# A decoder layer's routed experts on one core: gate and up computed by features, with copied weights and later sums

## Chip, core, metric

The kernel runs on one core of a Trainium2 chip. The metric is device time in microseconds (us) from start to end of one execution; lower is better. The profile's engines are TensorE (PE, with its weight loads PEld), VectorE (DVE), ScalarE (ACT), GpSimd (POOL) and SyncE (SP), which issues most DMAs here.

## What is computed

One pre-norm decoder layer over 16 sequences of 256 tokens with 256 features, all in fp32: self-attention with 16 heads, an additive cross term, and a mixture of experts. The change touches only the last of the three:

```python
def _moe(x, gate_w, w_gate, w_up, w_down, ws_gate, ws_up, ws_down):
    shared = silu(x @ ws_gate) * (x @ ws_up) @ ws_down
    scores = sigmoid(x @ gate_w.T)                 # 16 experts
    topk_w, topk_idx = top_k(scores, 2)
    topk_w = topk_w / (topk_w.sum(-1, keepdims=True) + 1e-20) * 2.5
    route = zeros((T, 16)).at[arange(T)[:, None], topk_idx].set(topk_w)
    g = einsum('th,ehm->etm', x, w_gate)           # h = 256, m = 128
    u = einsum('th,ehm->etm', x, w_up)
    eo = einsum('etm,emh->eth', silu(g) * u, w_down)
    return einsum('te,eth->th', route, eo) + shared

x = x + attention(layernorm(x))
x = x + cross(layernorm(x), ctx)
x = x + _moe(layernorm(x), ...)
```

The kernel computes only the two chosen experts of each token. It needs 2 x 4,096 expert rows.

## The kernel before

**First stage (up to some 364 us of the profile).** Attention, the cross term, routing and the shared expert of sequences 0 to 11 run as a software pipeline over the sequences, in an order written out by hand. Every normalised token row (256 features and 8 more columns: two weights, a code of the first expert, the row's number; `ROW` = 264) is scattered twice to a DRAM list, `listed`, so that the rows of one expert stand together in blocks of 128. Blocks are padded to full ones: at most `NB` = 79, of which `USUAL` = 74 are always computed, and the other five only if they are needed (`unusual_blocks`, L1018). `owner_row` holds the expert of each block.

**Block stage.** Class `Block` (L268 to L346) does one block:

- its constructor loads 128 rows of `listed` on SP's queue (132 KB);
- `turn` (L280): two TensorE transposes bring the features to the partitions, ScalarE copies them to `rowsT`;
- `pick` (L288): three VectorE instructions on 128x1 elements choose the row's weight and its destination;
- `hidden_product` (L304): gate and up together. The turned rows are the stationary operand, the expert's weights the moving one, 256 columns (gate and up), two steps of contraction. Tokens lie on the partitions of the result `gu`. ScalarE applies Silu to the gate half;
- `weigh` (L316): VectorE multiplies by the row's weight and by up;
- `turn_hidden` (L323): a third transpose, and VectorE's copy `hidT`, bring the 128 hidden features to the partitions;
- `give` (L329): the down product, ScalarE's copy `got` out of PSUM, and an indirect DMA on GpSimd's queue that scatters the 128 result rows to `given`, one row for each token and choice.

The expert's weights are read from `wgu_sb` and `wd_sb` at an address in a register; `expert_of` (L348) loads the expert numbers of four blocks at a time into TensorE's registers.

**The loop (L1180 to L1206).** Its order is kept as written. Step i does `hidden_product` of block i-2, `turn_hidden` of i-3, `give` of i-4, `turn` of i, `weigh` of i-2, `pick` of i, at most one sum, at a due step one `fetch`, and the row load of block i+9 (`AHEAD`). The first six blocks' rows are loaded before the loop (L1008) into space that is free by then.

**Sums.** `fetch(b)` (L1091) loads both choices of sequence b's 256 tokens from `given` (512 KB, SP's queue), after all scatters up to block `lasts[b]` have landed; the last sequence's comes as two DMAs, one for each tile of 128 tokens. `add` (L1116) adds one 128x256 piece into `x_all` on VectorE; there are four for each sequence. `due` gives the step of each fetch: 25, 29, ... 65 for sequences 0 to 10, then 67, 71, 75, 78, 79. Its sums come `FETCHED` = 6 steps later, one per step. When all of a sequence's sums are done, its output DMA goes out (`added`, L1107).

**Shared expert of the last four sequences.** `SharedLate` (L1123): `gate_up` and `down`. The first `gate_up` stands in step 76, between the last `turn_hidden` and the last `give`s; all else stands behind the loop (L1212 to L1221), with the remaining sums.

PSUM in this stage: two buffers each for `tp`, `gu`, `th` and `eo`. In SBUF, among others, 14 `rows` (one block each), 4 `sum`, 6 `got`.

Of the kernel before, what the change touches and what calls it, by code (L numbers as in the profile page):

```python
# [76 lines left out]
def decoder_kernel(  # L77
# [188 lines left out]
    codes = None  # L266

    class Block:  # L268
        def __init__(self, i, home, rows=None, rowsT=None):
            self.i, self.home, self.rowsT = i, home, rowsT  # L270
            self.rows = self.tile("rows", [P, ROW]) if rows is None else rows
            ins = nc.sync.dma_start(out=self.rows, in_=listed[ts(i, P)])
            behind(ins, enlisted)
            enlisted.clear()
# [13 lines left out]
        def pick(self):  # L288

            code, own = self.rows[:, D + 2 : D + 3], codes[:, self.i : self.i + 1]  # L290
            self.weight = self.tile("weight", [P, 1])
            self.dest = self.tile("dest", [P, 1], I32)
            nc.vector.scalar_tensor_tensor(
                self.weight, code, own, self.rows[:, D : D + 1], ALU.is_equal, ALU.mult
            )
            nc.vector.scalar_tensor_tensor(
                self.dest, code, own, self.rows[:, D + 3 : D + 4], ALU.is_equal, ALU.add
            )

            nc.vector.tensor_tensor(  # L300
                self.weight, self.weight, self.rows[:, D + 1 : D + 2], ALU.max
            )

        def hidden_product(self, e):  # L304
            self.e = e
            gu = self.gu = self.tile("gu", [P, 2 * M])
            for k in range(KT):
                nc.tensor.matmul(  # L308
                    gu, lhsT=self.rowsT[:, k],
                    rhs=wgu_sb[:, ds(e, 1), k].rearrange("p a i m -> p (a i m)"),  # L310
                    start=(k == 0), stop=(k == KT - 1),
                )
            self.hid = self.tile("hid", [P, M])
            nc.scalar.activation(self.hid, gu[:, 0:M], AF.Silu)  # L314

        def weigh(self):  # L316

            nc.vector.scalar_tensor_tensor(  # L318
                self.hid, self.hid, self.weight, self.gu[:, M : 2 * M],
                ALU.mult, ALU.mult,  # L320
            )

        def turn_hidden(self):  # L323
            th = self.tile("th", [P, M])
            nc.tensor.transpose(th, self.hid, ident)  # L325
            self.hidT = self.tile("hidT", [M, P])
            nc.vector.tensor_copy(self.hidT, th)  # L327

        def give(self):  # L329
            eo = self.tile("eo", [P, D])  # L330
            nc.tensor.matmul(  # L331
                eo, lhsT=self.hidT,
# [4 lines left out]
            nc.scalar.copy(got, eo)  # L337
# [10 lines left out]
    def expert_of(i, n=1):  # L348

        _, values = nc.values_load_multi_w_load_instructions(  # L350
            owner_row[:, i : i + n], engines=(mybir.EngineType.PE,), min_val=0, max_val=E - 1,
            skip_runtime_bounds_check_because="a block's owner is one of E experts",
        )
        return values
# [5 lines left out]
    with tc.tile_pool(name="work", bufs=2) as work, tc.tile_pool(  # L360
# [644 lines left out]
        def begin_blocks():  # L1005

            nonlocal codes
            for i in range(6):  # L1008
                rows = h3T[:, i % KT, ds(first_free[i // KT] * TB * P, ROW)]
                blocks.append(Block(i, None, rows))  # L1010
# [7 lines left out]
        def unusual_blocks():  # L1018
# [3 lines left out]
                hidT=(work, "m2", 2), got=(work, "qT", 2), weight=(small, "v2", 4),  # L1022
                dest=(small, "dest", 2), tp=(p_sc, "sc", 2), gu=(p_sc, "sc", 2),
                th=(p_sc, "sc", 2), eo=(p_sc, "sc", 2),
# [5 lines left out]
            with tc.If(used > USUAL):  # L1030
                for i in range(USUAL, NB):
# [3 lines left out]
                    block.hidden_product(expert_of(i)[0])  # L1035
                    block.weigh()
                    block.turn_hidden()
# [49 lines left out]
    with tc.tile_pool(name="ew", bufs=3) as ew, tc.tile_pool(  # L1087
# [3 lines left out]
        def fetch(b):  # L1091

            got = ew.tile([P, TT, 2, D], F32, tag="sum", name="sum", bufs=4)
            parts = [(nc.sync, ts(b, TT), got)]
            if b == B - 1:
# [27 lines left out]
        class SharedLate:  # L1123
# [4 lines left out]

            def gate_up(self):

                ps = p_e.tile([P, 2, T], F32, tag="gu", name="late_ps")
                for i in range(2):
                    for k in range(KT):
                        nc.tensor.matmul(
                            ps[:, i], lhsT=wgu_sb[:, E, k, i], rhs=h3T[:, k, ts(self.b, T)],
                            start=(k == 0), stop=(k == KT - 1),
                        )
                self.hid = ew.tile([P, T], F32, tag="late", name="late", bufs=4)
                nc.scalar.activation(self.hid, ps[:, 0], AF.Silu)
                nc.vector.tensor_tensor(self.hid, self.hid, ps[:, 1], ALU.mult)  # L1140

            def down(self):
                for t in range(TT):
                    eo = p_e.tile([P, D], F32, tag="eo", name="late_eo")
# [10 lines left out]
        AHEAD, LANDED, FETCHED = 9, 3, 6  # L1155
# [4 lines left out]
        for b in range(B):  # L1160
# [3 lines left out]
            step = last + 4 + (LANDED if last + 4 < USUAL - AHEAD else 1)  # L1164
# [6 lines left out]
            rows=(ew, "rows", 14), rowsT=(ew, "rowsT", 3), hid=(ew, "hid", 3), hidT=(ew, "hidT", 3),  # L1171
            got=(ew, "got", 6), weight=(ew, "weight", 4), dest=(ew, "dest", 12), tp=(p_e, "tp", 2),
# [7 lines left out]
        for i in range(max(due) + 1):  # L1180
# [6 lines left out]
            if 3 <= i < USUAL + 3:  # L1187
                blocks[i - 3].turn_hidden()
# [66 lines left out]
```

## Time and profile before

| | |
|---|---|
| median of 6 runs | 508.34 us (505.42 to 509.58) |
| the profiled execution | 508.4 us, span of its instructions 506.6 us |
| mean granted TensorE clock in it | 0.990 |
| first stage, to the first matmul of block 0 | 364.4 us |
| blocks 0 to 73, first gate matmul to the last block's | 120.2 us |
| from there to the end | 22.0 us |

Busy time of each engine in the stretches of the block stage (columns: stretch, its length, then busy us and number of instructions of PE, PEld, DVE, ACT, POOL; the granted clock, the share in which the DMA engines were busy, GB/s):

```profile
372.00:392.00 20.00, 20.00 (x113) 16.91 (x112) 10.91 (x64) 11.55 (x38) 11.66 (x12) 1.00 0.54 167
422.00:432.00 10.00, 10.00 (x57) 8.40 (x56) 7.52 (x38) 5.67 (x19) 6.11 (x7) 1.00 0.88 298
442.00:452.00 10.00, 10.00 (x57) 8.46 (x57) 7.52 (x40) 5.78 (x20) 4.99 (x6) 1.00 0.88 295
452.00:462.00 10.00, 9.22 (x49) 7.28 (x48) 6.50 (x33) 4.80 (x17) 5.97 (x6) 1.00 0.78 244
484.56:506.62 22.06, 13.65 (x61) 10.62 (x59) 13.46 (x38) 3.30 (x9) 4.08 (x5) 0.93 0.55 170
```

A matmul in fp32 shows as two instructions, a transpose as one. Matmuls overlap in their ends, so their pace is read from start to start.

### The profile page before, as it was taken

To read this page: it belongs to the slowest core of one execution; us is meant where nothing else is said; L and a number is where in the kernel's file an instruction comes from. 1 tells how busy PE (TensorE), PEld (TensorE's weight loads), DVE (VectorE), ACT (ScalarE), POOL (GpSimd) and SP (SyncE) were. 2 spreads that over 40 slices of the span, in tenths; PEclk is the share of its full clock that TensorE was granted. 3 is DMA by queue.
4 is the path that set the end of the run, shared out by engine and by line. 5 is a ranking of instruction groups with operands and counts; after the bars stand their busy time and mean duration, and the time that the engine had idled before them with its cause. 6 is when DMAs were issued, how large, how long until landed. Compare 5 with 4: busy or idle time off the path is not lost. (4 is left out here: it accounts for less than half of the span.)

```text
span 506.6 us, 12732 instructions
## 1 busy us (share of the span) xinstructions
PE 472.3 (93%) x4078; PEld 315.6 (62%) x4078; DVE 386.4 (76%) x1607; ACT 329.4 (65%) x783; POOL 321.3 (63%) x539
## 2 busy tenths in 40 slices
PE   1899999999999999999999999998799999999993
PEld 0455656656556556556556655455588888887882
DVE  5845557879989989989989877997655567767765
ACT  2378789888787887888888898221255555555530
POOL 5765345687887887887886655676055566555640
PEclk9999999999999999999999999998899999999998
DMA  7796551342423423320200111112465376978755
GB/s 211 242 343 214 170 170 34 103 130 66 127 84 107 127 82 110 127 97 33 76 34 23 56 41 47 53 45 75 130 204 168 104 243 229 291 250 269 262 159 167
DMA packets 61139, 69.68 MB, mean 138 GB/s; under 512 B 7164, under 2 KB 52493, under 8 KB 61072
## 3 DMA queue, kind: packets, MB, share of 16 engines
q1 hardware_dynamic: 53760, 50.88, 33.2%
q0 software_dynamic: 6624, 17.05, 9.1%
q10 hardware_dynamic: 688, 0.92, 0.5%
q8 instruction: 34, 0.56, 0.4%
q14 instruction: 33, 0.27, 0.2%
HBM read 36.89 MB, written 33.24 MB: 138 GB/s over the span
## 5 line engine op out<-in xcount | busy, mean ns | idle before, releaser
L655 ACT ACTIVATE a<-sc 128x1024 f32<-128x1024 f32 x128 | 124.6, 1030 | 25.2 <-PE sc L645 24.4
L338 POOL DMA_INDIRECT given<-block_got,block_dest x74 | 72.7, 982 | 64.2 <-ACT block_rowsT L286 39.9
L901 POOL DMA_INDIRECT listed<-h,slots x64 | 66.8, 1044 | 16.3 <-issue 15.8
L645 PE MATMUL sc<-qT,kT 32*128 32x256 f32 x1024 | 75.7, 401 | 0.9 <-ACT a L655 0.9
L308 PE MATMUL block_gu<-wgu_sb,block_rowsT 128*128 x288 | 74.4, 381 | 0.3 <-ACT block_rowsT L286 0.3
L645 PEld LDWEIGHTS sc<-qT,kT 32*128 32x128 f32 x1024 | 47.4, 184 | 31.2 <-ACT kT L589 9.1
L665 PE MATMUL av<-a,vaug 128*32 128x256 f32 x1024 | 65.8, 381 | 0.1
L549 PE MATMUL pq<-wqkv,hT 128*128 128x512 f32 x128 | 63.2, 619 | 0.7 <-ACT hT L539 0.7
L327 DVE COPY block_hidT<-block_th 128x128 f32<-128x128 f32 x74 | 21.5, 291 | 41.5 <-PE block_th L325 22.0
L571 POOL TENSOR_TENSOR qkr<-rot,m 128x512 f32<-128x512 f32 x32 | 41.0, 1286 | 17.6 <-DVE m L565 9.5
L308 PEld LDWEIGHTS block_gu<-wgu_sb,block_rowsT 128*128 128x128 f32 x288 | 49.2, 190 | 4.7 <-ACT block_rowsT L286 0.5
L381 POOL TENSOR_TENSOR rs<-rs,neg_half 128x2 f32<-128x2 f32 x64 | 48.1, 752 | 5.3
L331 PE MATMUL block_eo<-wd_sb,block_hidT 128*128 x148 | 44.1, 381 | 0.0
L665 PEld LDWEIGHTS av<-a,vaug 128*32 128x32 f32 x1024 | 29.3, 110 | 21.3 <-issue 6.3
L314 ACT ACTIVATE block_hid<-block_gu 128x128 f32<-128x128 f32 x74 | 20.6, 278 | 33.8 <-PE block_gu L308 12.0
L387 POOL TENSOR_SCALAR h<-x_all,neg,rs 128x256 f32<-128x256 f32 x64 | 40.0, 629 | 3.4
L337 ACT COPY block_got<-block_eo 128x256 f32<-128x256 f32 x74 | 27.5, 372 | 21.3 <-issue 14.1
L676 ACT ACTIVATE xs<-av,vsum 128x256 f32<-128x256 f32 x64 | 27.2, 485 | 16.4 <-PE av L665 16.4
L559 DVE TENSOR_TENSOR rot<-pq,cosf 128x512 f32<-128x512 f32 x32 | 21.9, 686 | 17.3 <-PE pq L549 17.2
L549 PEld LDWEIGHTS pq<-wqkv,hT 128*128 128x128 f32 x128 | 22.6, 196 | 19.0 <-issue 16.7
L529 PE MATMUL tp_h<-ident,h 128*128 128x128 f32 x128 | 19.7, 287 | 11.8 <-POOL h L387 11.7
L597 PE MATMUL pv<-wqkv,hT 128*128 128x256 f32 x128 | 30.4, 380 | 0.1
(190 smaller groups left out, 991.9 us busy)
## 6 DMA issues: line engine op xcount, KB each, us to landing
listed<-empty SPq DMA_DIRECT2D x9, 1056.0 KB
block_rows<-listed SPq DMA_DIRECT2D x68, 132.0 KB
sum<-given SPq DMA_DIRECT2D x15, 512.0 KB
x_all<-in_x_dram SPq DMA_DIRECT2D x16, 256.0 KB
c<-in_ctx_dram SPq DMA_DIRECT2D x16, 256.0 KB
out_dram<-x_all SPq DMA_DIRECT2D x15, 256.0 KB
enc_row<-enc_rows SPq DMA_DIRECT2D x16, 128.0 KB
wgu_sb<-in_L_ffn_w_gate_dram SPq DMA_DIRECT2D x16, 128.0 KB
```

Source lines behind the costliest of these rows:

```text
L308: nc.tensor.matmul(gu, lhsT=self.rowsT[:, k], rhs=wgu_sb[:, ds(e, 1), k].rearrange("p a i m -> p (a i m)"), start=(k == 0), stop=(k == KT ...
L331: nc.tensor.matmul(eo, lhsT=self.hidT, rhs=wd_sb[:, ds(self.e, 1)].rearrange("m a d -> m (a d)"), start=True, stop=True,)
L338: ins = nc.gpsimd.indirect_dma_start(out=given, out_offset=bass.IndirectOffsetOnAxis(ap=self.dest, axis=0), in_=got, in_offset=None, bound ...
L381: nc.gpsimd.tensor_tensor(r, r, neg_half, ALU.pow)
L387: nc.gpsimd.tensor_scalar(h[:, t, 0:D], src[:, t], neg[:, t : t + 1], r[:, t : t + 1], ALU.add, ALU.mult)
L549: nc.tensor.matmul(pq.rearrange("p h i two -> p (h i two)"), lhsT=self.hT[:, k, ts(t, P)], rhs=wqkv[:, k, 0 : 2 * D], start=(k == 0), stop ...
L571: nc.gpsimd.tensor_tensor(self.qkr[:, t], self.rot[t].rearrange("p h d -> p (h d)"), self.m2[t].rearrange("p h i two -> p (h i two)"), ALU ...
L597: nc.tensor.matmul(self.pv[:, t], lhsT=self.hT[:, k, ts(t, P)], rhs=wqkv[:, k, 2 * D : 3 * D], start=(k == 0), stop=(k == KT - 1),)
L645: nc.tensor.matmul(scs[j // 2][:, j % 2, kt], lhsT=self.kT[rows, g % 2, g // 2, ts(kt, P)], rhs=self.qT[rows, g // 2], start=True, stop=True,)
L655: nc.scalar.activation(a, self.scs[g][i], AF.Square, bias=1.0, scale=HD**-0.5)
L665: nc.tensor.matmul(self.av[ts(j, 32), g % 2], lhsT=self.va[:, kt, head], rhs=self.a[g, j // 2][:, j % 2, kt], start=(kt == 0), stop=(kt == ...
L901: ins = nc.gpsimd.indirect_dma_start(out=listed, out_offset=bass.IndirectOffsetOnAxis(ap=self.slots[:, i, t : t + 1], axis=0), in_=self.h3 ...
```

## The change

**Gate and up by features.** `hidden_product` swaps its operands: the expert's weights, 128x128 at a time, are stationary, and the turned rows move, 128 columns. Two halves (gate, up) times two steps of contraction make four matmuls, with hidden features on the partitions of the result. `turn_hidden` and `hidT` go, and so does the step between: `give` of block i-3 now stands in step i.

**Copied weights.** A new `weights` copies the expert's gate and up weights (128x512) on VectorE into a tile `w` with a fixed address (four buffers), in step i for block i. `expert_of` loads the numbers into VectorE's registers too.

**The row's weight.** With tokens no longer on the partitions of the hidden tile, `weigh` becomes `gated` (hidden times up), and `give` multiplies by the weight as ScalarE copies the down product out of PSUM.

**Rows and picking by groups of four.** A new class `Group` loads four blocks' rows in one DMA (528 KB, five buffers) and picks all four blocks' weights and destinations in four VectorE instructions on 128x4 elements, at the first of the four. The first six blocks remain groups of one.

**Later sums.** `FETCHED` goes from 6 to 9, `sum` from four buffers to five; fetches are due one step earlier in number (24, 28, ... 64, 66, 70, 74, 77, 78), as `give` is.

**The end.** `late[0]`'s gate stands before the last block's `give`, its up behind it. The last two sequences are fetched by token tile. `late[3].down` moves ahead of the last sequence's sums. PSUM: two `tp`, three `gu`, three `eo`.

```diff
+    GROUP = 4
+    class Group:
+        def __init__(self, i, n, home, rows=None):
...
+                self.rows = self.tile("rows", [P, n, ROW])
+            ins = nc.sync.dma_start(
+                out=self.rows, in_=listed[i * P : (i + n) * P].rearrange("(n p) d -> p n d", p=P)
+            )
...
+        def pick(self):
...
+            first, second, code, last = (self.rows[:, :, D + i] for i in range(4))
+            own = codes[:, self.i : self.i + self.n]
...
+            nc.vector.tensor_tensor(same, code, own, ALU.is_equal)
+            nc.vector.tensor_tensor(self.weight, same, first, ALU.mult)
+            nc.vector.tensor_tensor(self.weight, self.weight, second, ALU.max)
+            nc.vector.tensor_tensor(self.dest, same, last, ALU.add)
...
-        def hidden_product(self, e):
+        def weights(self, e):
             self.e = e
-            gu = self.gu = self.tile("gu", [P, 2 * M])
-            for k in range(KT):
-                nc.tensor.matmul(
-                    gu, lhsT=self.rowsT[:, k],
-                    rhs=wgu_sb[:, ds(e, 1), k].rearrange("p a i m -> p (a i m)"),
-                    start=(k == 0), stop=(k == KT - 1),
-                )
-            self.hid = self.tile("hid", [P, M])
-            nc.scalar.activation(self.hid, gu[:, 0:M], AF.Silu)
-        def weigh(self):
-            nc.vector.scalar_tensor_tensor(
-                self.hid, self.hid, self.weight, self.gu[:, M : 2 * M],
-                ALU.mult, ALU.mult,
-            )
-        def turn_hidden(self):
-            th = self.tile("th", [P, M])
-            nc.tensor.transpose(th, self.hid, ident)
-            self.hidT = self.tile("hidT", [M, P])
-            nc.vector.tensor_copy(self.hidT, th)
+            self.w = self.tile("w", [P, KT, 2, M])
+            nc.vector.tensor_copy(self.w.unsqueeze(1), wgu_sb[:, ds(e, 1)])
+        def hidden_product(self):
+            gu = self.gu = self.tile("gu", [M, 2, P])
+            for i in range(2):
+                for k in range(KT):
+                    nc.tensor.matmul(
+                        gu[:, i], lhsT=self.w[:, k, i], rhs=self.rowsT[:, k],
+                        start=(k == 0), stop=(k == KT - 1),
+                    )
+            self.hid = self.tile("hid", [M, P])
+            nc.scalar.activation(self.hid, gu[:, 0], AF.Silu)
+        def gated(self):
+            nc.vector.tensor_tensor(self.hid, self.hid, self.gu[:, 1], ALU.mult)
...
-                eo, lhsT=self.hidT,
+                eo, lhsT=self.hid,
...
-            nc.scalar.copy(got, eo)
+            nc.scalar.activation(got, eo, AF.Copy, scale=self.weight)
...
-            owner_row[:, i : i + n], engines=(mybir.EngineType.PE,), min_val=0, max_val=E - 1,
+            owner_row[:, i : i + n], min_val=0, max_val=E - 1,
+            engines=(mybir.EngineType.PE, mybir.EngineType.DVE),
...
-            got = ew.tile([P, TT, 2, D], F32, tag="sum", name="sum", bufs=4)
+            got = ew.tile([P, TT, 2, D], F32, tag="sum", name="sum", bufs=5)
...
-            if b == B - 1:
+            if b >= B - 2:
...
-        AHEAD, LANDED, FETCHED = 9, 3, 6
+        AHEAD, LANDED, FETCHED = 9, 3, 9
...
-            step = last + 4 + (LANDED if last + 4 < USUAL - AHEAD else 1)
+            step = last + 3 + (LANDED if last + 3 < USUAL - AHEAD else 1)
...
+            if i < USUAL:
+                blocks[i].weights(expert[i])
             if 2 <= i < USUAL + 2:
-                blocks[i - 2].hidden_product(expert[i - 2])
+                blocks[i - 2].hidden_product()
+            if i == USUAL + 2:
+                late[0].product(0)
             if 3 <= i < USUAL + 3:
-                blocks[i - 3].turn_hidden()
+                blocks[i - 3].give()
             if i == USUAL + 2:
-                late[0].gate_up()
-            if 4 <= i < USUAL + 4:
-                blocks[i - 4].give()
+                late[0].product(1)
             if 2 <= i < USUAL:
                 blocks[i].turn()
             if 2 <= i < USUAL + 2:
-                blocks[i - 2].weigh()
+                blocks[i - 2].gated()
+            if i == USUAL + 2:
+                late[0].gated()
...
-            if i + AHEAD < USUAL:
-                blocks.append(Block(i + AHEAD, home))
+            load_blocks(i + AHEAD + 1)
...
         tail_adds(B - 2)
+        late[3].down()
         tail_adds(B - 1)
-        late[3].down()
```

`load_blocks(end)` makes groups of four until `end` blocks are begun.

## The prediction

> **What bounds the kernel now.** I read four views. First the chain of work that ended last, on the page (shares of the span):
>
> ```profile
> PE 24%; DMA 2%; DVE 1%; issue 0%; POOL 0%; DVEq 0%; POOLq 0%; ACT 0%; SPq 0%
> PE block_gu L308 12%; PE block_eo L331 6%; PE block_tp L283 4%; PE block_th L325 2%; DMA given<-block_got,block_dest 1%; DMA sum<-given 1%; DVE x_all L1120 1%; PE shared_eo L942 0%; POOL given L338 0%; DVE block_hid L318 0%; DVE block_hidT L327 0%; DVE x_all L949 0%; DVEq L1251 0%; ACT h3T L286 0%; POOLq L1251 0%
> ```
>
> Then the same chain in order of time, one block of it (start, length):
>
> ```profile
> 446.98 0.87 PE block_gu L308 x4
> 447.85 0.11 PE block_th L325
> 447.96 0.43 PE block_eo L331 x2
> 448.39 0.22 PE block_tp L283 x2
> ```
>
> Then the timeline, for what lies beside such a block and for the last sums (start, length, engine, line):
>
> ```profile
> 437.07 0.21 DVE L293 SCALAR_TENSOR_TENSOR block_weight<-block_rows,h3T 128x1 f32<-128x1 f32 x1
> 437.20 0.21 DVE L296 SCALAR_TENSOR_TENSOR block_dest<-block_rows,h3T 128x1 int32<-128x1 f32 x1
> 437.33 0.15 DVE L300 TENSOR_TENSOR block_weight<-block_weight,block_rows 128x1 f32<-128x1 f32 x1
> 437.40 0.42 DVE L1120 TENSOR_TENSOR x_all<-x_all,sum 128x256 f32<-128x256 f32 x1
> 437.68 0.98 POOL L338 DMA_INDIRECT given<-block_got,block_dest  x1 [0.65 <-ACT block_rowsT L286]
> 438.23 0.29 DVE L327 COPY block_hidT<-block_th 128x128 f32<-128x128 f32 x1 [0.41 <-issue]
> 438.44 0.34 DVE L318 SCALAR_TENSOR_TENSOR block_hid<-block_hid,block_weight,block_gu 128x128 f32<-128x128 f32 x1
> ...
> 502.73 0.74 DVE L1149 TENSOR_TENSOR x_all<-x_all,late_eo 128x256 f32<-128x256 f32 x2
> ```
>
> Last, four lines' own instructions, as prices for VectorE (min/median/max ns):
>
> ```profile
> L446 DVE TENSOR_SCALAR tri<-tri,pcol x1: 277/277/277, 13.8 to 13.8; 128x128 f32<-128x128 f32 x1
> L692 DVE STREAM_TRANSPOSE xt<-xs x32: 667/670/714, 45.0 to 318.8; 128x512 f32<-128x512 f32 x32
> L864 DVE TENSOR_SCALAR ends_new<-count x16: 163/175/244, 93.0 to 346.6; 128x16 f32<-128x16 f32 x16
> L510 DVE SCALAR_TENSOR_TENSOR junk_c<-c,mlp_bc x32: 405/426/2008, 15.1 to 270.0; 128x256 f32<-128x256 f32 x32
> ```
>
> In the block stage the chain is TensorE alone: gate and up 0.87, turn of the hidden tile 0.11, down 0.43, turn of the next rows 0.22, together 1.63 us for each block. The matmuls of block 0 start at 364.37, those of block 73 at T = 484.56; most blocks lie 1.63 apart. Around 455, 466 and 472 the gaps are longer, 2.15 us in all, with no landing named as late. VectorE works some 1.2 of 1.63 us when the sums run, ScalarE 1.02 (L314 0.28, L337 0.37, L286 0.37), GpSimd 0.98. After T come 22.0 us; VectorE's last op ends at 503.47 = T + 18.9 and the last output lands 3.1 later.
>
> **TensorE, per block.** The turn goes: -0.109 (start to start of th and eo, 380.958 to 381.067). Gate and up stay 1,024 columns, but go from 4 passes of 256 (0.866) to 8 passes of 128, with a weight load each. Which is longer, the load or the columns? Two turns with 128 columns lie 0.108 apart; the two passes of `po` (L1012, 128 weights, 128 columns, fp32) start 0.110 apart; the passes of `ahead` (L796, 32 columns, so the load alone sets their pace) 0.112. I take `po`, which has this very shape: 8 x 0.110 = 0.880. Net -0.109 + 0.014 = -0.095, block time 1.53; by the two other rows -0.111 and -0.079. Over 73 intervals: **-6.9** (-8.1 to -5.8). The dynamic address moves from TensorE to VectorE's copy; TensorE keeps one, for down.
>
> **VectorE, per block.** Gone: hidT, the weighing, three tiny ops. Kept: one sum of 0.40 (8 in 3.27). Added: a gating product, between L327's start-to-start 0.21 and L318's 0.26, taken as 0.24; four tiny ops per group of four, each waiting for the one before (such ops start 0.21 apart, L864 to L867): 0.2 per block (four per block for the first six); a load of expert numbers, 0.55 per four blocks as TensorE's own, 0.14; an address, 0.05. And the weights' copy, 128x512 from SBUF to SBUF, which this trace does not show. Upper bound: L692 moves as much in 0.670. Lower: `tri` (L446), the only large one-source elementwise op from SBUF to SBUF, takes 0.277 for 128 columns and the same form 0.228 for 8 (L422): 0.41 ns a column, so 0.43 for 512. I take 0.43, because L446 is elementwise and L692 a transpose; 0.38 start to start. Sum 0.38 + 0.24 + 0.20 + 0.40 + 0.14 + 0.05 = 1.41, under 1.53: cost 0, hidden by TensorE. With 0.63 for the copy it is 1.66 and VectorE is the bound while sums run (41 blocks): +0.13 x 41 = +5.3. A copy is issued two iterations before its use with four buffers, so its lateness shows only when the total exceeds TensorE's.
> [...]
>
> **The shared port, the strongest case against.** [...] L510 (two SBUF inputs) takes 0.426 in the median, but 2.008 where it ran into GpSimd's work (195.05, with an L571 beneath). While only scatters run, L745 stays at 0.45 to 0.49 and the sums at 0.42; but L864, a small one-source op, went from 0.175 to 0.244 in such places. I take 0; the bounds are no hold and half a scatter (0.49) per copy.
> [...]
>
> **ScalarE.** Multiplying the weight into the eviction makes L337 an activation with a column operand; L676, such a one of the same shape, takes 0.485 against 0.372: 1.14 of 1.53, no cost. GpSimd has 0.56 spare.
>
> **SP and DMA.** 68 row loads become 17 of 528 KB: 51 issues of 0.4 fewer. Per four blocks 528 KB rows, 512 sums, 512 scatter, 256 output = 1.85 MB; at 6.12 us 302 GB/s, against 286 at 0.88 busy now (422 to 452). Sums are fetched one step earlier in number, at the same distance from the scatter, and used 9 steps later instead of 6: the fetch at 454.88 was issued 8.1 us after its step began, held by the scatter's landing, and landed 3.8 later, against 6 x 1.63 = 9.8; nine are 13.8. Behind it in SP's queue lies the row group, needed 9 steps after its place: lag 7.1, landing 4.3 (as the row loads now) + 396 KB more at 327 GB/s (286/0.88) 1.2 = 12.6, under 13.8. Cost 0, thin cover: if it is gone, TensorE's turn waits for rows.
>
> **Start.** Gate of block 0 now starts when VectorE's last L949 ends (364.27); copy 0 comes after it: +0.5 (0 to 1.0 with the load of numbers exposed).
>
> **The 2.15 us of long gaps** I leave in (0 to -2.2), as nothing in the change names their cause.
>
> **After the last block.** TensorE from T: gu 0.88, down of 72 0.43, late gate 0.87, down of 73 0.43: ends T + 2.6 (before T + 4.5, as th waited and late gate and up stood before both downs). Eviction and scatter: GpSimd done T + 4.6 (before 491.75, T + 7.2); fetches issue at T + 8.3 instead of T + 10.9 and land from T + 11 to T + 13.5. But VectorE isn't there yet. More sums are left over: with 9 steps to wait, 3 fall into the last iterations and 18 behind, where there were 4 and 15. From late gating at T + 3.7 on it has 3 + 18 + 8 down sums at 0.40 = 11.6, four gatings at 0.41 = 1.6 and one wait of 0.6 for the next gate's matmuls: T + 17.5. Then 3.1 for the output: T + 20.6, **-1.4**. So VectorE takes the place of the scatter, and fetching by token tile brings nothing. Bounds: landing-bound -4, more waits +1.
>
> **Sum** against the profiled execution (span 506.6, time 508.4; the median of the six runs, 508.34, is the same): -6.9 + 0.5 + 0 - 1.4 = -7.8: **500.6 us**. Own range 496 to 504.
>
> **Rivals.**
> *VectorE becomes the bound* (copy at L692's pace): +5.3, 505.9. For it: no copy of this size in the trace. Against: L446.
> *Slower: the copy waits for GpSimd's descriptors.* With 0.49 per block VectorE needs 1.90, in the 41 blocks with sums: 41 x (1.90 - 1.53) = +15.2, 515.8. It decides from a wait of 0.31 (0.19 over 1.53 in 41 blocks eats the 7.8). For it L510's 2.008 and L864's 0.244; against it L745 and the sums beside scatters.
> *Row groups land late*: 1 us in each of some ten groups under load: +10, 510.6. For it the thin 1.2 us; against it, that rows now land 3.4 to 4.3 after issue, evenly.
> That the change doesn't do what it says is unlikely: the turn and its copy are gone from the code.
>
> **From this to the numbers.** Forecast 0.64, VectorE 0.14, port 0.12, rows 0.07, the rest 0.03. Time 500.6. Range 495 (gaps vanish, tail bound by landing) to 507 (VectorE's case included). About 0.5%, 2.5 us, is what a measurement of this kernel can tell: faster means under 505.8, with the forecast, half of VectorE's case and a third of the rows' case that costs less: 0.78; within 0.5% 0.10; slower 0.12.
>
> **What would show it.** Gate and up passes 0.110 apart and blocks 1.53 apart with TensorE without gaps: the first step right. The copy's duration near 0.43, and whether it lengthens beside a scatter, decides two rivals. VectorE idle before the gating means TensorE still leads. Turns waiting for rows mean the third. In the tail, sums running back to back to about 18 us after the last gate. Blocks more than 1.66 apart would make it wrong.

## The result, and the profile after

The changed kernel takes 512.28 us (median of 20 runs, 509.96 to 517.02), the kernel before 507.67 beside it (46 runs): ratio 1.0103, 95% interval 1.0082 to 1.0123. It is 1% slower, where 500.6 was forecast. Its profiled execution has a span of 513.2 us, against 506.6 before. The medians lie 4.6 us apart, these two executions 6.6. Where the 6.6 us went, by the starts of the block matmuls (L308 before, L340 after):

| stretch | before | after | difference | forecast |
|---|---|---|---|---|
| start to block 0 | 364.37 | 368.54 | +4.2 | +0.5 |
| block 0 to block 73, at the median pace | 73 x 1.628 | 73 x 1.546 | -6.0 | -6.9 |
| what single blocks take above that pace | 2.05 | 11.87 | +9.8 | 0 |
| block 73 to the end | 22.0 | 20.4 | -1.6 | -1.4 |

(The two rows of the block stage come to 0.5 to 0.7 us more than its 120.19 and 124.23 us, as intervals under the median aren't counted against them.) Of the +4.2 some 3.0 is there long before the change begins: the first scatter to `listed` starts at 100.74 instead of 97.72, which no other profile of the changed kernel shows (97.56 to 97.74), though those of two variants do in part (100.53 and 99.63). So it belongs to the single execution. The other 1.2 is the start of the block stage. The pace, the end and the start went about as worked out, and the gaps made the difference. (Gaps here and below are what the intervals take above their median, where that is over 0.1 us.)

In the page's chain VectorE's share has gone from 1% to 3% and ScalarE's from 0% to 1%, for the gating product L349 and the Silu L345 among others:

```profile
PE 24%; DVE 3%; ACT 1%; issue 0%; DVEq 0%
PE block_gu L340 11%; PE block_eo L353 7%; PE block_tp L317 5%; DVE x_all L1143 1%; DVE block_hid L349 1%; PE late_ps L1157 1%; ACT block_hid L345 1%; DVE x_all L1179 1%; PE shared_eo L965 0%; DVE late L1165 0%; DVEq L333 0%; DVE block_w L333 0%; ACT late L1164 0%; ACT h3T L320 0%; DVE x_all L972 0%
```

Three of its costliest groups (busy us and mean ns, then the engine's idle time before them and what ended most of it):

```profile
L360 POOL DMA_INDIRECT given<-block_got,block_dest x74 | 76.5, 1034 | 63.6 <-ACT block_rowsT L320 44.8
...
L353 PE MATMUL block_eo<-wd_sb,block_hid 128*128 x148 | 46.4, 395 | 6.5 <-DVE block_hid L349 6.5
...
L333 DVE COPY block_w<-wgu_sb 128x512 f32 x74 | 33.9, 458 | 2.6 <-issue 1.9
```

TensorE's down product waits 6.5 us for the gating product. Before, the same kind of wait came to 0.9 us, for the turn of the hidden tile (us in total, times, longest):

```profile
PE block_th L325 <- DVE block_hid L318: 0.9, 3, 0.5
```

From start to start of the matmuls the loss before down is 8.7 us, and 2.1 more lie between down's two passes, which start 0.32 instead of 0.22 apart 21 times. VectorE itself isn't late: the view of the tile `block_hid` has it waiting for ScalarE's Silu, and ScalarE waiting for TensorE (idle us of the engine, times):

```profile
L349 DVE TENSOR_TENSOR block_hid<-block_hid,block_gu x74: 267/289/290, 370.1 to 494.6; 128x128 f32<-128x128 f32 x74
its engine sat idle before it (us, times) until:
  ACT block_hid L345: 39.4, 42
  PE block_tp L317: 19.1, 15
  DVE block_hid L349: 15.7, 27
  PE block_gu L340: 13.2, 24
```

One gap in the timeline (start, length, engine, line; in brackets idle time before and releaser):

```profile
429.03 1.06 PE L340 MATMUL block_gu<-block_rowsT,block_w 128*128 128x128 f32 x8
...
429.78 1.23 POOL L360 DMA_INDIRECT given<-block_got,block_dest  x1 [0.30 <-issue]
...
429.92 0.60 PE L353 MATMUL block_eo<-wd_sb,block_hid 128*128 x2
430.08 0.42 DVE L333 COPY block_w<-wgu_sb 128x512 f32 x1
...
430.57 1.06 PE L340 MATMUL block_gu<-block_rowsT,block_w 128*128 128x128 f32 x8
...
431.40 0.28 ACT L345 ACTIVATE block_hid<-block_gu 128x128 f32<-128x128 f32 x1 [1.65 <-PE block_tp L317]
431.57 0.47 ACT L359 ACTIVATE block_got<-block_eo,block_weight 128x256 f32<-128x256 f32 x1
431.71 0.29 DVE L349 TENSOR_TENSOR block_hid<-block_hid,block_gu 128x128 f32<-128x128 f32 x1 [1.21 <-ACT block_hid L345]
...
432.05 0.70 PE L353 MATMUL block_eo<-wd_sb,block_hid 128*128 x2 [0.42 <-DVE block_hid L349]
```

Block 37's gate and up end at 430.09 and ScalarE is free, but its Silu starts at 431.40, 1.31 late; on the chip with the second line below it follows in 0.04 (median). TensorE meanwhile went on in time: down of block 36, the next turn and the next gate and up. What came late was not its work but the signal that it was done. The trace's own records of the semaphore that TensorE counts up, around that place, and two blocks' worth of them from the last set of runs below, on another chip:

```
changed, first profile:   431.37 431.42 431.46 431.65
changed, last set:        420.71 421.15 421.37   422.26 422.69 422.91
```

The second line is the usual rhythm: one signal each for gate and up, down and the turn. In the first, the three that belong to ends at 430.09, 430.52 and 430.74 come 0.04 to 0.05 apart; the fourth, of block 38's gate and up (431.63), is in time again. From block 34 on this comes about every third block, costs TensorE some 0.65 us each time, and 23 of 74 Silus start over 0.2 us late. In the kernel before 4 did, and three of them stand at its "long gaps" (blocks 55, 61 and 64; the fourth cost nothing). Its signals come in bunches there too: 466.51, 466.54, 466.58, 466.63.

In the end part VectorE's last sum ends at 510.34, 17.6 us after block 73's start, as worked out (17.5).

### The profile page after: what moved, and what is told of

Same layout as the page of the kernel before. It is cut to its first block, busy times and chain, and to the rows that moved or that the text cites. A ratio compares the mean times of both kernels' runs of the same rounds, so it can differ in the third digit from the quotient of the medians.

```text
span 513.2 us, 12866 instructions
## 1 busy us (share of the span) xinstructions
PE 472.1 (92%) x4300; PEld 323.9 (63%) x4300; DVE 382.9 (75%) x1477; ACT 333.1 (65%) x783; POOL 325.9 (64%) x539
## 5 line engine op out<-in xcount | busy, mean ns | idle before, releaser
L360 POOL DMA_INDIRECT given<-block_got,block_dest x74 | 76.5, 1034 | 63.6 <-ACT block_rowsT L320 44.8
L340 PE MATMUL block_gu<-block_rowsT,block_w 128*128 128x128 f32 x576 | 76.7, 276 | 0.0
L340 PEld LDWEIGHTS block_gu<-block_rowsT,block_w 128*128 128x128 f32 x576 | 70.0, 192 | 1.2 <-ACT block_rowsT L320 0.6
L349 DVE TENSOR_TENSOR block_hid<-block_hid,block_gu 128x128 f32<-128x128 f32 x74 | 21.1, 286 | 47.8 <-ACT block_hid L345 39.4
L353 PE MATMUL block_eo<-wd_sb,block_hid 128*128 x148 | 46.4, 395 | 6.5 <-DVE block_hid L349 6.5
L345 ACT ACTIVATE block_hid<-block_gu 128x128 f32<-128x128 f32 x74 | 20.9, 283 | 42.6 <-PE block_tp L317 19.1
L359 ACT ACTIVATE block_got<-block_eo,block_weight 128x256 f32<-128x256 f32 x74 | 35.1, 474 | 14.2 <-PE block_eo L353 6.2
L333 DVE COPY block_w<-wgu_sb 128x512 f32 x74 | 33.9, 458 | 2.6 <-issue 1.9
```

The source lines that it names most:

```text
L340: nc.tensor.matmul(gu[:, i], lhsT=self.w[:, k, i], rhs=self.rowsT[:, k], start=(k == 0), stop=(k == KT - 1),)
L353: nc.tensor.matmul(eo, lhsT=self.hid, rhs=wd_sb[:, ds(self.e, 1)].rearrange("m a d -> m (a d)"), start=True, stop=True,)
L359: nc.scalar.activation(got, eo, AF.Copy, scale=self.weight)
L360: ins = nc.gpsimd.indirect_dma_start(out=given, out_offset=bass.IndirectOffsetOnAxis(ap=self.dest, axis=0), in_=got, in_offset=None, bound ...
```

## The experiments

For each run "late" is the number of Silus that start over 0.2 us after both their gate and up and ScalarE's last instruction have ended, "gaps" the excess of the block intervals over their median, as above. These runs came in five sets, each on another chip. On two of the chips the kernel before takes about 507 us, as in the first runs, on three about 502; this turned out to matter. In the prediction and the expectations "shared port" and "port" name the theory that VectorE's copy and GpSimd's scatter hold each other, and "GpSimd's descriptors" the scatter's instruction on GpSimd (0.98 us in the median of the first profile); no run shows a port, or what GpSimd does in that time.

**One step more between gate and up and down.**

```diff
-            if 3 <= i < USUAL + 3:
-                blocks[i - 3].give()
+            if 4 <= i < USUAL + 4:
+                blocks[i - 4].give()
-            step = last + 3 + (LANDED if last + 3 < USUAL - AHEAD else 1)
+            step = last + 4 + (LANDED if last + 4 < USUAL - AHEAD else 1)
-            hid=(ew, "hid", 3)
+            hid=(ew, "hid", 4)
```

> The changed kernel with down of a block one step later (i-4 for i-3; hid with four buffers, due steps one later). In the changed kernel's trace TensorE's matmuls end on time, but the silu that follows them starts up to 1.28 us late every third block, because the increments of TensorE's semaphore arrive late and in a bunch; the gating product follows, and down waits 0.65 us for it. Theory 'too little slack' (late signals do harm only because one step, some 1.3 us, lies between gate and up and down): gaps above the median pace fall from 12.0 us to under 3, block stage 120.19 -> about 115, time about 503 (ratio to the kernel before 0.99). Theory 'TensorE itself is held' (the late signals come of a stall of its own): gaps stay near 12, time 512 to 514. Theory 'shared port': the copy is still held, time 512.

Measured: 496.68 beside 502.60 for the kernel before, ratio 0.9868 (0.9835 to 0.9901); none late.

**Rows in single transfers.**

```diff
-            ins = nc.sync.dma_start(out=self.rows, in_=listed[i * P : (i + n) * P]...)
+            for j in range(n):
+                ins = nc.sync.dma_start(out=self.rows[:, j], in_=listed[ts(i + j, P)])
...
```

> The changed kernel with each group's rows in four transfers of 132 KB again, all else as changed. Theory 'row groups' (528 KB bursts fill the DMA queues and hold the scatters or the sums, or crowd what carries the signals): gaps fall from 12.0 to under 4, time about 504. Rivals (density of TensorE's instructions, shared port, slack): no difference, 511 to 514, with 51 more transfers on SP's queue.

Measured on the same chip: 496.53, 0.9858 (0.9813 to 0.9904); none late.

**No copy of the weights.** The choice of the expert for gate and up is left out.

```diff
-            self.w = self.tile("w", [P, KT, 2, M])
-            nc.vector.tensor_copy(self.w.unsqueeze(1), wgu_sb[:, ds(e, 1)])
...
-                        gu[:, i], lhsT=self.w[:, k, i], rhs=self.rowsT[:, k],
+                        gu[:, i], lhsT=wgu_sb[:, 0, k, i], rhs=self.rowsT[:, k],
```

> The changed kernel without the weights' copy: gate and up of every block read expert 0's weights where they lie, so the choice of the expert for gate and up is left out; VectorE's loads of the numbers stay. [...] Theory 'density' (24 records of TensorE per 1.545 us, late signals whatever VectorE does): gaps of 0.65 every third block stay, time 511 to 512.

Measured on the same chip: 495.59, 0.9851 (0.9804 to 0.9898); none late.

**The kernel before with short passes.**

```diff
-            for k in range(KT):
-                nc.tensor.matmul(gu, lhsT=self.rowsT[:, k], rhs=wgu_sb[:, ds(e, 1), k]...)
+            for i in range(2):
+                for k in range(KT):
+                    nc.tensor.matmul(gu[:, ts(i, M)], lhsT=self.rowsT[:, k],
+                                     rhs=wgu_sb[:, ds(e, 1), k, i]...)
```

> The kernel before with gate and up in 8 passes of 128 columns instead of 4 of 256, rows still stationary, all else as before. By pass length alone 8 x 0.112 - 0.866 = +0.03 per block, +2 us, time 510. Theory 'density' (the signals come late when TensorE has so many short instructions): gaps above the median pace, 2.2 us in the kernel before, grow to 8 or more, time 516 or more. Rivals (port, row groups): gaps stay near 2, time 509 to 511.

Measured on the same chip: 502.75, 1.0016 (0.9989 to 1.0043); none late, pace 1.655 against 1.628.

What follows: three unlike edits each seemed to cure the same thing, and no theory had expected it of all three. The changed kernel itself had not run beside them, and the kernel before was 1% faster there than at first. So nothing was shown yet but that a control was missing.

**The control, the kernel before, and the sums at six steps again.** The first two are the two kernels, unchanged; the third:

```diff
-            got = ew.tile([P, TT, 2, D], F32, tag="sum", name="sum", bufs=5)
+            got = ew.tile([P, TT, 2, D], F32, tag="sum", name="sum", bufs=4)
-        AHEAD, LANDED, FETCHED = 9, 3, 9
+        AHEAD, LANDED, FETCHED = 9, 3, 6
```

> The changed kernel itself once more, as the control for the three variants that all came out 1.3 to 1.5% under the kernel before: one step more of slack (496.7), rows in single transfers (496.5), no weights' copy (495.6), beside 502.6 for the kernel before; the first stage was shorter there too (block 0 starts at 360.6 instead of 368.5). Theory 'each of the three edits took away the gaps': this kernel is again 1% slower than the kernel before (ratio 1.01), gaps above the median pace near 12 us. Theory 'the gaps belong to the chip or to the placement of that run and not to the three edits': this kernel too comes out 1.3 to 1.5% faster, ratio 0.985, with gaps under 3 us.

> The kernel before as a run of its own, for its trace beside the others: ratio 1.00; block stage 120.2 and gaps near 2 us as in its first profile; block 0 starts near 359 if the chip is as the last one, near 364 if it is as the first.

> The changed kernel with the sums used 6 steps after their fetch again, with four buffers, as before. Theory 'gaps belong to the chip': the same as the changed kernel beside it, or 2 us faster or slower by waits for sums. Theory 'later sums make the gaps': 0.985 while the changed kernel shows 1.01.

Measured, beside 507.87 for the kernel before: changed kernel 505.37, 0.9957 (0.9926 to 0.9988), 13 late, gaps 6.15; kernel before 506.57, 1.0011 (0.9977 to 1.0045), 1 late, gaps 2.47; sums at six steps 504.29, 0.9961 (0.9933 to 0.9990), 9 late, gaps 6.87. The same kernel that was 1% slower is 0.4% faster here, with half of the gaps. The later sums make no difference that is clear of noise.

**Four kernels on one chip of the 507 kind.** The first three as above; in the fourth GpSimd's scatter is replaced by a plain write on SP's queue, so the placing of the rows by token is left out:

```diff
-            ins = nc.gpsimd.indirect_dma_start(out=given, out_offset=..., in_=got, ...)
+            ins = nc.sync.dma_start(out=given[ts(self.i % 64, P)], in_=got)
...
```

> The changed kernel again, now on one chip with three variants: so far 1.010 of the kernel before (first result) and 0.996 (beside the kernel before as a run of its own), with 11.9 and 6.2 us of gaps. The silu starts over 0.2 us late after 23 and 13 blocks' gate and up there, and after none in the four variants of the other call. If the size of the gaps belongs to the chip, it lies anywhere from 0.985 to 1.010 here, and only the variants beside it tell.

> The changed kernel with down one step later. Theory 'late signals of TensorE become gaps because one step lies between gate and up and down': signals as late as in the changed kernel beside it, but gaps at least 4 us fewer, if that one has 6 or more. Theory 'TensorE is held': the same gaps as the changed kernel.

> The changed kernel without the weights' copy (gate and up of every block use expert 0's weights, the choice of the expert is left out). Theory 'the copy against GpSimd's descriptors makes the signals late': none late, gaps near 0, 6 us or more under the changed kernel beside it if that one has such gaps. Theory 'the copy has no part': as many late signals as the changed kernel.

> The changed kernel with a plain write of each block's rows on SP's queue in place of GpSimd's scatter: the placing of the rows by token is left out. In the late cases TensorE's signals come 0.3 us after the end of a scatter's work on GpSimd (443.92 to 444.20, 478.96 to 479.22). Theory 'late signals come of GpSimd's descriptors': none late, gaps of that kind gone, stage near 113 us. Theory 'density of TensorE's instructions': late signals stay as in the changed kernel. SP's queue has one more issue per block, so a wait for rows or sums may show.

| beside 507.21 | time | ratio | late | gaps | block stage |
|---|---|---|---|---|---|
| changed | 512.61 | 1.0100 (1.0069 to 1.0130) | 26 | 14.4 | 127.2 |
| a step more | 512.72 | 1.0103 (1.0058 to 1.0148) | 24 | 9.2 | 126.1 |
| no copy | 507.52 | 1.0003 (0.9972 to 1.0033) | 23 | 9.3 | 121.9 |
| no scatter on GpSimd | 498.58 | 0.9855 (0.9808 to 0.9902) | 0 | 0 | 112.3 |

This set decides three things. The late signals need GpSimd's scatters: without them none is late, on a chip where three kernels beside it have 23 to 26, and TensorE runs 73 blocks without a gap. (Which part of a scatter does it, GpSimd's own work or the transfer of single rows on its queue, this edit doesn't separate.) The two groups' lines of that run:

```profile
L353 PE MATMUL block_eo<-wd_sb,block_hid 128*128 x148 | 44.2, 380 | 0.0
L345 ACT ACTIVATE block_hid<-block_gu 128x128 f32<-128x128 f32 x74 | 20.5, 277 | 31.2 <-PE block_gu L340 31.2
```

The copy has a part in the price, though hardly in the count: without it 5.1 us come back, 5.3 in the block stage of the two profiles. That the copy alone delays the signals is refuted: without it 23 Silus are late, with it 26. And one step more before down doesn't help. Down then waits for nothing, but ScalarE, held up by the late signals, also comes late to `rowsT` (0.70 us after the turn's end in the median, 0.19 on the quiet chip below), and gate and up wait for that instead (a median pace of 1.647, which is why the gaps look smaller). More room between the turn and gate and up was not tried. Of that run, down's group, and from the view of the tile `block_gu` what its engines waited for (the last line is TensorE's, weight loads and matmuls counted each):

```profile
L353 PE MATMUL block_eo<-wd_sb,block_hid 128*128 x148 | 44.2, 380 | 0.0
...
its engine sat idle before it (us, times) until:
  ACT block_hid L345: 39.0, 37
  PE block_gu L340: 29.7, 25
  issue: 18.6, 24
  ACT block_rowsT L320: 18.1, 38
```

**What in the change multiplies them?** Four kernels: short passes in the kernel before, single rows, a turn more, and the complement (row groups, group picks, later sums and fetches as changed; gate and up, and the order at the end, as before). The third's edit:

```diff
-            for k in range(KT):
+            for k in (0, 0, 1):
                 nc.tensor.transpose(tp[:, k], self.rows[:, ts(k, P)], ident)
```

> The kernel before with gate and up in 8 passes of 128 columns, again, on another chip (the time of the kernel before tells which kind: 502.6 beside no late signals, 507 to 508 beside many). By pass length alone 1.005. Theory 'a denser run of TensorE's instructions, together with GpSimd's scatters, makes its completion signals late' (the changed kernel has 25 records of TensorE per 1.545 us, the kernel before 22 per 1.628, this one 32 per 1.655): more late signals than the kernel before's 1 to 4, at least 10, ratio 1.015 or more on a chip of the 507 kind. Rival 'what the change does elsewhere (row groups, copy, sums, one step less)': at most 5 late, ratio 1.005.

> The changed kernel with the groups' rows in four transfers again. On a chip of the 507 kind: theory 'row groups make the signals late': under 5 late, gaps under 4 us, ratio 0.985 to 0.99. Theory 'density and scatter': 20 or more late, gaps of 10 us or more, ratio 1.01. On a chip of the 502 kind it shows nothing (0.986).

> The changed kernel with the first half of each block's rows turned twice (one more load and pass, +0.11 us per block on TensorE, the same result): pace 1.655 as slow as the kernel before's, with as many of TensorE's records per us as the changed kernel. By passes alone +8.0 us on the changed kernel. Theory 'the pace matters: scatters of 0.98 us every 1.545 us': the late signals fall to the kernel before's 1 to 4, so part of the 8.0 us is given back, ratio near 1.005. Theory 'density': as many late as the changed kernel, though with the same lateness; ratio 1.02 to 1.025 on a chip of the 507 kind.

> The complement: the kernel before with the change's row groups, group picks, later sums and fetch by token tile, but gate and up, weighing and turn of the hidden tile as before, and the order at the end as before. Theory 'gate and up by features bring the late signals': as few late as in the kernel before (1 to 4), ratio 0.995 to 1.00. Theory 'row groups or sums bring them': 10 or more late, ratio over 1.005.

This set met a chip of the other kind (501.34 for the kernel before), and no run had a late signal, so it leaves the question open. Measured: short passes 502.36, 1.0021 (1.0002 to 1.0040); single rows 495.53, 0.9871 (0.9844 to 0.9899); a turn more 502.77, 1.0025 (1.0002 to 1.0048), at a pace of 1.655; the complement 502.28, 1.0012 (0.9991 to 1.0033). The complement shows that row groups, later sums and fetches by tile bring nothing by themselves there; by difference, the gain on such chips is that of gate and up by features, with the order at the end.

**Once more, with the changed kernel.**

> The changed kernel once more. On chips where the kernel before takes 501 to 503 us its variants showed no late signal and 0.985 to 0.987; this kernel itself has not run there. If it lands on such a chip: theory 'the late signals belong to those chips, and without them the forecast holds' expects ratio 0.985 to 0.990, gaps under 3 us, block stage near 114 us. On a chip of the 507 kind: 0.995 to 1.010 and 6 to 14 us of gaps, as in its three runs so far.

> The kernel before with 8 passes of 128 columns. On a chip of the 507 kind, theory 'number of TensorE's instructions': 10 or more late signals, ratio 1.015 or more; rival 'not the number, but pace, copy or row groups': at most 5 late, ratio 1.005 or less. On a chip of the 502 kind: 1.002, as twice so far.

> The changed kernel with the first half of the rows turned twice, pace 1.655. On a chip of the 507 kind, theory 'pace' (a scatter of 1 us every 1.545 us leaves too little time between two scatters): at most 5 late, ratio near 1.003, so faster than the changed kernel beside it though TensorE has more to do. Theory 'copy, row groups or number of instructions': as many late as the changed kernel, ratio 1.015 or more. On a chip of the 502 kind: 1.0025, as before.

Again the other kind (502.80). The changed kernel takes 496.68, ratio 0.9900 (0.9858 to 0.9941), with none late and no gap: its block stage is 112.35 us. Short passes 502.60, 1.0016 (0.9988 to 1.0043); a turn more 504.86, 1.0043 (1.0015 to 1.0072). Four stretches of the block stage (from:to, length, PE busy with its number of records, then PEld, DVE, ACT, POOL) first of the changed kernel in its first profile, then in this one:

```profile
370.00:400.00 30.00, 30.00 (x230) 27.70 (x230) 16.44 (x73) 19.07 (x58) 18.25 (x18) 1.00 0.55 182
400.00:430.00 30.00, 28.92 (x212) 25.71 (x211) 15.66 (x60) 16.82 (x53) 17.68 (x19) 1.00 0.56 191
430.00:460.00 30.00, 28.12 (x208) 25.32 (x208) 19.73 (x69) 16.38 (x51) 17.25 (x17) 1.00 0.74 253
460.00:492.00 32.00, 28.99 (x212) 25.83 (x211) 19.81 (x69) 16.98 (x54) 19.45 (x18) 1.00 0.69 218
```

```profile
361.00:388.00 27.00, 27.00 (x212) 25.29 (x212) 15.43 (x69) 17.67 (x53) 16.52 (x17) 1.00 0.60 195
388.00:415.00 27.00, 27.00 (x211) 25.20 (x210) 14.50 (x56) 17.50 (x53) 17.57 (x18) 1.00 0.56 168
415.00:442.00 27.00, 27.00 (x213) 25.29 (x212) 19.32 (x73) 17.93 (x53) 16.02 (x18) 1.00 0.88 292
442.00:471.00 29.00, 29.00 (x228) 27.09 (x227) 21.00 (x75) 18.86 (x57) 19.73 (x20) 1.00 0.88 280
```

The granted clock (the column before the last two, DMA share and GB/s) is 1.00 in all eight. On the first chip TensorE begins almost without a gap and loses time from 400 on; on this one it never stops. And this one's timeline, with the same kernel, has every Silu at its place and the scatters evenly 1.55 apart:

```profile
420.37 0.97 POOL L360 DMA_INDIRECT given<-block_got,block_dest  x1 [0.46 <-ACT block_rowsT L320]
...
420.74 0.28 ACT L345 ACTIVATE block_hid<-block_gu 128x128 f32<-128x128 f32 x1 [0.38 <-PE block_gu L340]
...
421.92 0.97 POOL L360 DMA_INDIRECT given<-block_got,block_dest  x1 [0.57 <-ACT block_rowsT L320]
...
422.28 0.28 ACT L345 ACTIVATE block_hid<-block_gu 128x128 f32<-128x128 f32 x1 [0.38 <-PE block_gu L340]
```

**Settled and open.** Shown, for executions that are recorded as all of these were: on some chips TensorE's signals come late (by up to 1.8 us in the first profile); GpSimd's scatters are needed for it; the copy adds to its price; neither a step more before down nor the earlier sums cure it. On the one chip without late signals on which the changed kernel itself ran, the change is worth 1.0% (0.6 to 1.4). In the three sets of runs of the 507 kind, the first included, it cost 1.0% twice and gained 0.4% once, so the kind doesn't settle the size.

Argued only: that a signal is held by the scatter at hand, and why it comes every third block. The expectation above has the signals 0.3 us after a scatter's end; over the 23 late Silus of the first profile the last recorded signal came anywhere from 0.56 us before the end of the latest scatter to 1.00 after it. In that profile 34 of 73 scatters follow the one before within 0.35 us, as the two at 428.50 and 429.78, on the quiet chip 8. The author's guess is that bunched signals let two results go at once, so that two scatters run back to back and hold the next signals longer. That pattern may be effect as well as cause.

Open: what in the change multiplies the late signals, since the kernel before scatters as much and has 1 to 4. The number of TensorE's instructions, the pace and the row groups never ran apart on a chip that shows them. Open too is what differs between the chips, and whether the recording has a part. The traces of the 507 kind hold 15 to 18 semaphore records for each block of the changed kernel (blocks 35 to 70), the quiet ones, and the run without GpSimd's scatters, 36 to 37. So in these runs late signals and missing records stand in the same traces. No run was made without the recording, and none shows whether one has to do with the other. No complete kernel was shown to beat the kernel before on both kinds of chip; the one with single rows ran only on the quiet kind, the one with sums at six steps only on the other.

## Why the prediction was wrong

**The failed step** is the sentence "The 2.15 us of long gaps I leave in (0 to -2.2), as nothing in the change names their cause." They were the visible end of late signals of TensorE, which the change multiplies. They grew to 11.9 us in the first profile, 6.15 and 14.4 in two others, and to nothing on the chips without late signals. The sum needed a term of 9.8 us there and had 0. Not knowing a cause was taken as a reason for "no change", and the bounds had only a lower side. The rows for a warning were there: in those gaps no landing was late, ScalarE was idle, and TensorE's work had ended. Why the change makes so many more of them stays open.

**TensorE's pace** was right in kind. Passes come 0.1117 us apart, not 0.110, so 8 x 0.0017 = 0.014 of the block time was missed: 1.546 instead of 1.53, and -6.0 us instead of -6.9, within the bounds. Without the gaps the measured terms make -6.0 + 1.2 - 1.6 = -6.4; where no signal was late the medians differ by 496.68 - 502.80 = -6.1.

**The start** was undersized: 1.2 us instead of 0.5, above its bound of 1.0. VectorE's last sum before it ends at 367.27, then come 0.64 us in which VectorE shows no work, the first copy (0.43) and block 0 at 368.54. The first load of expert numbers (L372, 0.36) isn't in the 0.64: it starts at 366.59, beside that sum. Eight semaphore instructions of the copy's line, which the profile doesn't count as work, start from 367.14 to 367.81, of 0.02 to 0.05 each. **The tail** was right: -1.6 against -1.4, and VectorE bound it as worked out.

**VectorE.** The copy's 0.43 from row L446 was right: 0.42 in the median (0.458 in the mean of the first profile), and VectorE waited for the Silu before 56 of the 74 gating products of the quiet run, so it isn't the bound. The sum L1143, with two sources, takes 0.419 for 256 columns, the copy 0.42 for 512; no run varies the copy's width, so the 0.41 ns a column stays an estimate from L446 and L422.

**Copy and scatter.** The rival of a copy held by half a scatter (0.49) didn't occur in that size. On the quiet chip 18 copies lie wholly inside a scatter and take 0.418 in the median, the scatters 0.972. But copy and scatter take longer where they meet at certain places, and in the first profile they meet there far more often: 14 of its 74 copies take 0.49 to 0.65, on the quiet chip one. Two such pairs of the first profile:

```profile
426.93 0.42 DVE L333 COPY block_w<-wgu_sb 128x512 f32 x1
426.99 1.20 POOL L360 DMA_INDIRECT given<-block_got,block_dest  x1 [1.71 <-ACT block_rowsT L320]
...
427.80 0.65 DVE L333 COPY block_w<-wgu_sb 128x512 f32 x1
```

All 13 copies that start 0.58 to 0.81 us after a scatter's start are lengthened there, and a scatter that starts less than 0.27 us after a copy takes up to 1.21. Inside a scatter a copy can run at its usual 0.42, as the 18 show; at these places the two lengthen, by up to 0.23 us the copy and 0.26 the scatter. The views of TensorE's waits name no copy inside the block stage. The rival's sign came true on the chip with late signals, where the copy was worth 5.1 us; by which way it costs them isn't shown.

**Row groups and sums.** No gap on the quiet chip, so no wait for rows; the thin cover of 1.2 us held. That the sums' distance costs nothing was right, and it gains nothing either.

The chance of 0.12 for slower was given to the wrong mechanism, and the 0.78 for faster is more than the parts it names (0.64, half of 0.14 and a third of 0.07 make 0.73). All rivals concerned resources that the change uses more; none concerned how the end of work is told to the next engine.

## What to carry to other kernels

A gap in the profile whose cause isn't found belongs in the range with both signs: when an engine starts late though its input has ended and it is idle, ask when the signal arrived, and which engine's work lies across it. Put the unchanged candidate beside its variants in every set of runs: three variants looked like cures until the control ran on another chip. And a tuned schedule whose steps follow each other in 1.5 us is judged on several chips before 1% is believed.

## What the runs showed of the hardware

- TensorE's completion signals arrived late in three of six sets of runs, by up to 1.8 us in the first profile, in bunches 0.04 us apart, while TensorE itself went on; in the run without scatters on GpSimd, in one of these sets, none did.
- Chips differ, each seen in one set of runs: the kernel before took 507 to 508 us in three sets of runs and 501 to 503 in three. Some 4 us of that lie before the blocks: from the first scatter to `listed` to the last it takes 255.2 to 256.4 us in the first three and 251.8 to 252.0 in the others, in both kernels alike.
- On the 507 kind half of the semaphore records of the block stage are missing from the traces of the changed kernel (15 to 18 for each block, against 36 to 37 on the quiet chips); in the run without GpSimd's scatters they are there (36 to 37).
- A 128x512 copy on VectorE and a scatter on GpSimd took longer where they met in some phases (the copy as much as 0.65 us instead of 0.42, the scatter 1.23 instead of 0.97), and not in others (18 copies inside a scatter 0.418 in the median on the quiet chip).
